# The last expert tiles are added to the output in two column halves instead of whole rows

## The chip, the core and the metric

The kernel runs on one core of a Trainium2 chip. The metric is the device time of one execution in microseconds (us). Engines are named as the profile names them: PE (TensorE matmul), PEld (its weight load), DVE (VectorE), ACT (ScalarE), POOL (GpSimd) and SP (SyncE); a `q` after a name (POOLq) is that engine's own instruction sequencer.

## What is computed

The reference is a two-layer graph network followed by a routed feed-forward layer, on x with 1250 rows of 1024 floats:

```python
x = x + gnn(layernorm(x), src, dst, ...)          # two SAGE layers over 40,000 edges
t = layernorm(x)
logits = silu(t @ rw1 + rb1) @ rw2 + rb2          # 8 experts
vals, idx = top_k(logits, 2)                      # 2 experts per row
w = softmax(logits, only the two chosen)
eh = silu(einsum('td,edh->teh', t, ew1) + eb1)    # hidden size 256
eo = einsum('teh,ehd->ted', eh, ew2) + eb2
out = x + t + sum over e of w[t,e] * eo[t,e]
```

So each of the 1250 rows gets two expert results added, 2500 (row, expert) pairs in all.

## The kernel before

The graph part runs first (functions `gnn_windows` and `after_layers`). When it is done, `after_layers` has written the normalised rows to a DRAM scratch `t_d` and the base value x + t to `out`. The rest is `moe`: it routes every row, packs the 2500 pairs into tiles of 128 slots that each belong to one expert, and works tile by tile. `NTILE` is 27, `always` is 20: tiles 0 to 19 are always worked, the rest under a runtime branch on `n_tiles`, the count of tiles that this input needs. `ends` is [23, 25, 27]: one branch for tiles 20 to 22, one nested in it for 23 and 24, one more for 25 and 26. In the profiled execution 23 tiles are worked (23 scatters, L1608), so the first branch is entered and the second is not.

For tile i the steps are:

- `gather(i)` (L1547, POOL): an indirect DMA reads 128 rows of `t_d`. It is issued three tiles ahead.
- `fetch(i)` (L1558, L1561): PE transposes the tile, ACT copies it out of PSUM.
- `first_layer(i)` (L1575, L1581): PE multiplies by the expert's first weights; DVE copies the hidden rows.
- `turn_hidden(i)` (L1588, L1590): PE transposes them, ACT applies bias and silu.
- `second_layer(i)` (L1597 to L1608): ACT scales the expert's bias row; for each of the two column halves (512 columns) PE runs its matmuls (L1602) and DVE writes `yo = ps * w + yb` for that half (L1607). Then POOL issues one indirect DMA (L1608) that adds the 128 rows of `yo` to rows of `out`, with `compute_op=ALU.add`; the row of each slot stands in `to[:, i]`. Slots that hold no pair have an index beyond `bounds_check` and move no row.

`yo` has two buffers, `yos[i % 2]`. Rows may be added to by two different tiles, so each scatter waits until the one before it has landed in `out`. The plan of tiles 4 and up is made once, in `plan_rest`: its call of `tokens_of` (L1405 to L1416) writes the columns 4 to 26 of `to` with one DVE instruction (L1416).

Program order decides the order on each engine: `section` (a loop over tiles) issues for tile i the gather of i + 3, the fetch of i + 1, the hidden transpose of i - 1, the first layer of i, then the second layer of i - 1. PE and ACT follow this order as written (`manual_schedule`); on POOL gathers and scatters form one queue, in order. A branch is taken by every engine by itself: L1654 is the line of the `If` on `n_tiles`, L1727 that of the `If` on `ok` after all tiles, which skips a second, general version of the whole kernel, and L1759 is the end of the kernel. A DMA of POOL signals its landing on one of eight semaphores, DMASW0 to DMASW7; POOL's DMAs from `gather(0)` on take them in turn, 0 to 7 and again from 0. Where a branch is not entered, the program has instructions on the other side that wait on semaphores the skipped side would have used, and raise them by as much as it would have (the record `INC_SWDGE_SEM`), so that both sides leave the same counts.

Of the kernel before, what the change touches and what calls it, by code (L numbers as in the profile page):

```python
# [14 lines left out]
I32 = mybir.dt.int32  # L15
AF = mybir.ActivationFunctionType
ALU = mybir.AluOpType
# [4 lines left out]
P = 128  # L22
# [7 lines left out]
def kernel(  # L30
# [21 lines left out]
    nc = tc.nc  # L52
    N, D = x.shape
# [12 lines left out]
    NTILE = (2 * N) // P + E  # L66
    assert R * 2 * EG == NE and R <= P and 2 * NB * WIN <= 512 and N > WIN
    rows = [min(P, N - b * P) for b in range(NB)]
# [70 lines left out]
    def tt(o, a, b_, op):  # L139
        nc.vector.tensor_tensor(o, a, b_, op)  # L140
# [912 lines left out]
    def moe():  # L1053
        st = ExitStack()
# [75 lines left out]
        sel_b = keep([P, NB_B + 1, E], F16)  # L1130
        beg_a, full_a = keep([P, E]), keep([P, E])
        ids, to, eid = (keep([P, NTILE], I32) for _ in range(3))
        w_slot = keep([P, NTILE])
        all_i = keep([P, 1], I32)

# [8 lines left out]
        group, ready = [], []  # L1144
# [63 lines left out]
        sums = SC[:, 2048:].rearrange("p (a n) -> p a n", a=4)  # L1208
# [186 lines left out]
        def by_slot(cols, nb, n):  # L1395

            ps = tpp.tile([P, 4, P], F32, name="tp").rearrange("p a b -> p (a b)")[:, :n]
            todo = [(c, b) for c in range(2) for b in range(nb)]
            for c, b in todo:
                r = at_row_a[:, c, b, :] if b < NA_B else at_row_b[:, c, b - NA_B, :]  # L1400
                nc.tensor.matmul(
                    ps, r, cols(c, b), start=((c, b) == todo[0]), stop=((c, b) == todo[-1])
                )
            return ps

        def tokens_of(at_tile, nb, i0, i1, take):

            n = i1 - i0
            tok = take([P, 2, nb, n], F16)
            tt(tok, at_tile, token[:, None, :nb, None].to_broadcast([P, 2, nb, n]), ALU.mult)  # L1410
            pi = by_slot(lambda c, b: tok[:, c, b, :], nb, n)
            nc.vector.tensor_scalar(ids[:, i0:i1], pi, -1.0, 0.0, op0=ALU.add, op1=ALU.max)
            to_f = take([P, n])
            nc.vector.tensor_scalar(to_f, pi, 0.0, float(4 * NP), op0=ALU.is_equal, op1=ALU.mult)
            tt(to_f, to_f, pi, ALU.add)
            nc.vector.tensor_scalar(to[:, i0:i1], to_f, -1.0, None, op0=ALU.add)  # L1416


        def weights(b0, nb, sel, take):
# [36 lines left out]
        def plan_first():  # L1456
            take = carver(scratch)
            choose(0, NA_B, sel_a, take)
            take = carver(scratch)
            rank = ranks(NA_B, sel_a, take)  # L1460
            hi_, lo_ = shifted(rank, take)
            nc.vector.tensor_copy(full_a, hi_[:, NA_B, :])
            nc.vector.tensor_copy(j[:, :NA_B], hi_[:, :NA_B, :])
            row = take([P, NA_B, E])
            nc.vector.tensor_copy(row, lo_[:, :NA_B, :])
            by_choice(row, 0, NA_B, rw[:, :, :NA_B], take)
            one_hot_rows(at_row_a, 0, NA_B)
            s = sums_before(full_a, take)
            nc.vector.tensor_copy(beg_a, s)

            til = take([P, NA_B, E])
            tt(til, j[:, :NA_B], full_a[:, None, :].to_broadcast([P, NA_B, E]), ALU.is_ge)
            stt(til, til, float(4 * NTILE), j[:, :NA_B], op0=ALU.mult, op1=ALU.add)
            tt(til, til, beg_a[:, None, :].to_broadcast([P, NA_B, E]), ALU.add)
            end = take([P, E])
            tt(end, beg_a, full_a, ALU.add)
            tw = take([P, 2, NA_B])
            by_choice(til, 0, NA_B, tw, take)
            at_tile = one_hot_tiles(tw, NA_B, 0, NT_A, take)
            tokens_of(at_tile, NA_B, 0, NT_A, take)  # L1480
            experts_of(0, NT_A, end, take)
            return at_tile, take

        def plan_rest():
# [40 lines left out]
            at_tile = one_hot_tiles(tw, NB, NT_A, NTILE, take)  # L1525
            yield
            tokens_of(at_tile, NB, NT_A, NTILE, take_l)
            experts_of(NT_A, NTILE, tot, take_l)
            yield at_tile
# [65 lines left out]
        def second_layer(i, e, hT):  # L1595
            yo, yb = yos[i % 2], ybs[i % 4]
            nc.scalar.activation(yb, yb, AF.Copy, scale=w_slot[:, i : i + 1])  # L1597
            for h in range(2):
                dc = slice(h * HALF, (h + 1) * HALF)
                ps = mm2.tile([P, 512], F32, name="ps2")  # L1600
                for q in range(KH):
                    nc.tensor.matmul(  # L1602
                        ps, hT[:, q, :],
                        w2_all[:, ds(e, 1), q * D + h * HALF : q * D + (h + 1) * HALF],
                        start=(q == 0), stop=(q == KH - 1),
                    )
                stt(yo[:, dc], ps, w_slot[:, i : i + 1], yb[:, dc], op0=ALU.mult, op1=ALU.add)  # L1607
            nc.gpsimd.indirect_dma_start(  # L1608
                out=out[:, :],
                out_offset=bass.IndirectOffsetOnAxis(ap=to[:, i : i + 1], axis=0),  # L1610
                in_=yo, in_offset=None, bounds_check=N - 1, oob_is_err=False,
                compute_op=ALU.add,
            )

# [2 lines left out]
        always = -(-2 * N // P)  # L1617
# [4 lines left out]
        def section(i0, i1, joined=True, until=None, middle=None):  # L1622

            for i in range(i0, i1):
                if i + 3 < NTILE and i > 1:
                    gather(i + 3)
                ahead = i + 1 < (until or i1)
                if ahead:
                    spread_bias(i + 1)
                    xTs[i + 1] = fetch(i + 1)  # L1630
                rest = None
                if i > i0 or joined:
                    turned = turn_hidden(i - 1, *held.pop(i - 1))
                    rest = lambda: second_layer(i - 1, *turned)

                early = rest if not ahead and until is None else None
                held[i] = first_layer(i, xTs.pop(i), middle or early)
                if rest is not None and early is None:
                    rest()

        def sections(i0, ends):
            last = held.pop(i0 - 1)

            def end_of_last():
                second_layer(i0 - 1, *turn_hidden(i0 - 1, *last))

            if not ends:
                end_of_last()
                return

            joined = i0 == always
            if not joined:
                end_of_last()
            with tc.If(n_tiles > i0) as more:  # L1654
                spread_bias(i0)
                xTs[i0] = fetch(i0)
                if joined:
                    held[i0 - 1] = last
                section(i0, ends[0], joined)
                sections(ends[0], ends[1:])  # L1660
            if joined:
                with more.Else():
                    end_of_last()
# [60 lines left out]

    gnn_windows()
    ok = moe()
    with tc.If(ok == 0):  # L1727
        gnn_any()
        moe()
# [34 lines left out]
```

## Time and profile before

| | us |
|---|---|
| median of 3 runs | 1120.42 |
| the 3 runs | 1119.36, 1120.42, 6438.05 |
| the profiled execution's own time | 1118.35 |
| its span, first to last instruction | 1116.6 |
| PE busy | 1089.5 (98%) |
| POOL busy | 313.6 (28%) |
| scatters (L1608): POOL busy, count | 36.5, 23 |
| last DVE result of the last tile, end | 1100.98 |
| last scatter, start on POOL | 1103.25 |

The two times at the bottom are counted from the span's start. The span covers the instructions of one execution; the execution's own time is 1.75 us more. A scatter's record on POOL (1586 ns in the mean) is the issue; its landing is found in the chain of waits and in the table of DMA issues.

### The profile page before, as it was taken

To read this page: it belongs to the slowest core of one execution; us is meant where nothing else is said; L and a number is where in the kernel's file an instruction comes from. 1 tells how busy PE (TensorE), PEld (TensorE's weight loads), DVE (VectorE), ACT (ScalarE), POOL (GpSimd) and SP (SyncE) were. 2 spreads that over 40 slices of the span, in tenths; PEclk is the share of its full clock that TensorE was granted. 3 is DMA by queue.
4 is the path that set the end of the run, shared out by engine and by line. 5 is a ranking of instruction groups with operands and counts; after the bars stand their busy time and mean duration, and the time that the engine had idled before them with its cause. 6 is when DMAs were issued, how large, how long until landed. Compare 5 with 4: busy or idle time off the path is not lost.

```text
span 1116.6 us, 13639 instructions
## 1 busy us (share of the span) xinstructions
PE 1089.5 (98%) x4881; PEld 809.9 (73%) x4881; DVE 472.9 (42%) x1172; ACT 218.3 (20%) x511; POOL 313.6 (28%) x407
## 2 busy tenths in 40 slices
PE   8999999999999999999999999999999999999993
PEld 7556556888888888888888888887544577676761
DVE  8767777763121245342234142455522263222221
ACT  4522222101111101110010000023111133333331
POOL 2999898500000000022002211254000013232321
PEclk9999999999999999999999999999999999999997
DMA  8011011010100020033004270343960456677762
GB/s 260 12 39 40 1 38 39 2 38 1 38 1 1 1 76 19 1 114 126 22 1 154 96 269 7 105 171 147 334 207 1 160 180 180 183 182 192 192 172 47
DMA packets 62320, 107.37 MB, mean 96 GB/s; under 512 B 8906, under 2 KB 35690, under 8 KB 62240
## 3 DMA queue, kind: packets, MB, share of 16 engines
q1 hardware_dynamic: 51392, 79.69, 20.9%
q0 software_dynamic: 7056, 23.88, 9.2%
q10 hardware_dynamic: 3792, 2.79, 0.8%
q8 instruction: 43, 0.70, 0.3%
q14 instruction: 37, 0.30, 0.1%
HBM read 80.74 MB, written 27.42 MB: 97 GB/s over the span
## 4 chain that ended last, share of the span: by engine, by line
PE 74%; DMA 16%; DVE 4%; issue 3%; ACT 1%; POOL 1%; SPq 0%; POOLq 0%; ACTq 0%; DVEq 0%
DMA out_dram<-L 13%; PE ps L532 12%; PE ps L460 11%; PE psb L664 11%; PE ps L760 8%; PE ps L664 8%; PE ps L568 8%; PE ps L1230 4%; PE ps L1244 3%; PE cnt L421 3%; PE ps L1183 2%; DMA b_p<-in_L_gnn_b_dram 1%; DMA more<-in_L_gnn_W_self_dram 1%; DVE xw L140 1%; PE ps L1575 1%
## 5 line engine op out<-in xcount | busy, mean ns | idle before, releaser
L413 POOL TENSOR_SCALAR ol<-lane,keys 125x128 f16<-125x128 f16 x280 | 171.0, 628 | 31.8 <-ACT keys L230 22.3
L460 PE MATMUL ps<-h0T,L 128*128 128x498 f32 (+2 forms) x384 | 146.0, 514 | 0.2 <-ACT h0T L309 0.2
L532 PE MATMUL ps<-L,h0T 128*128 128x256 f32 (+1 forms) x640 | 142.2, 379 | 0.8 <-DVE yl L387 0.8
L756 POOL TENSOR_TENSOR L<-L 128x512 f32<-128x512 f32 (+1 forms) x20 | 28.2, 1417 | 393.5 <-DMA L<-in_x_dram 393.4
L532 PEld LDWEIGHTS ps<-L,h0T 128*128 128x128 f32 (+1 forms) x640 | 118.3, 187 | 19.0 <-DVE yl L387 1.1
L460 PEld LDWEIGHTS ps<-h0T,L 128*128 128x128 f32 x384 | 67.2, 190 | 38.7 <-issue 34.7
L418 DVE TENSOR_SCALAR oh<-win,keys 125x240 f16<-125x240 f16 x320 | 81.1, 307 | 29.7 <-PE cnt L421 28.0
L1575 PE MATMUL ps<-xw,L 128*128 x368 | 84.1, 380 | 0.7 <-issue 0.7
L1602 PE MATMUL ps<-xw,L 128*128 x184 | 82.8, 593 | 0.5 <-ACT L L1590 0.5
L568 PE MATMUL ps<-C,yh 128*128 128x256 f32 (+2 forms) x240 | 81.7, 355 | 0.0
L568 PE MATMUL ps<-C,yl 128*128 128x256 f32 (+2 forms) x240 | 81.4, 353 | 0.0
L760 PE MATMUL ps<-zh,C 128*128 128x512 f32 (+1 forms) x200 | 79.5, 398 | 0.0
L760 PE MATMUL ps<-zl,C 128*128 128x512 f32 (+1 forms) x200 | 78.6, 393 | 0.0
L1575 PEld LDWEIGHTS ps<-xw,L 128*128 128x128 f32 x368 | 68.0, 190 | 9.5 <-issue 1.4
L440 DVE TENSOR_TENSOR C<-C,cnt 128x240 f32 x160 | 64.4, 402 | 12.9 <-DVE C L440 1.3
L1608 POOL DMA_INDIRECT out_dram<-L x23 | 36.5, 1586 | 118.2 <-DVE L L1607 62.0
L1547 POOL DMA_INDIRECT L<-t_d,L x26 | 25.5, 980 | 143.7 <-DVE L L140 122.9
L1602 PEld LDWEIGHTS ps<-xw,L 128*128 128x128 f32 x184 | 34.9, 190 | 34.9 <-issue 32.3
L1607 DVE SCALAR_TENSOR_TENSOR L<-ps,L 128x512 f32<-128x512 f32 x46 | 34.5, 751 | 53.1 <-PE ps L1602 53.1
L664 PE MATMUL ps<-L 128*128 128x256 f32 x240 | 56.2, 379 | 0.0
L387 DVE TENSOR_TENSOR yl<-ps,yh 128x256 fp32r<-128x256 f32 (+1 forms) x40 | 16.9, 423 | 92.3 <-ACT yh L386 92.3
L421 PEld LDWEIGHTS <-ol 125*128 125x128 f16 x320 | 31.0, 97 | 34.3 <-POOL ol L413 16.5
(237 smaller groups left out, 1558.1 us busy)
## 6 DMA issues: line engine op xcount, KB each, us to landing
xw<-in_L_ffn_ew_dram SPq DMA_DIRECT2D x16, 1024.0 KB, 11.2
L<-in_L_ffn_eb_dram SPq DMA_DIRECT2D x23, 512.0 KB, 4.7
L<-in_x_dram SPq DMA_DIRECT2D x20, 256.0 KB, 2.6
v_d<-L SPq DMA_DIRECT2D x18, 256.0 KB, 2.0
xa<-v_d SPq DMA_DIRECT2D x18, 256.0 KB, 7.2
t_d<-L SPq DMA_DIRECT2D x9, 512.0 KB, 3.8
out_dram<-xa SPq DMA_DIRECT2D x9, 512.0 KB, 4.0
L<-in_L_gnn_W_self_dram SPq DMA_DIRECT2D x4, 1024.0 KB, 5.3
```

What stands on the lines that cost most here:

```text
L413: nc.gpsimd.tensor_scalar(ol[:, c, :], lane[:GP], k, None, op0=ALU.is_equal)
L418: nc.vector.tensor_scalar(oh, win[:GP], keys[:, 0, i * GC + c, r : r + 1], None, op0=ALU.is_equal)
L421: nc.tensor.matmul(ps[:, i, :GW], ol[:, i * GC + c, :], oh, start=(c == 0), stop=(c == GC - 1),)
L440: nc.vector.tensor_tensor(to, to.bitcast(F32), ps[:, i, :GW].rearrange("p (k w) -> p k w", k=NB), ALU.add,)
L460: nc.tensor.matmul(ps[:, :n], w[:, k, (d % 2) * P : (d % 2 + 1) * P], h0T[:, k, c0 : c0 + n], start=(k == 0), stop=(k == KD - 1),)
L532: nc.tensor.matmul(ps[:m, :QW], hT[:, k, blk(b)], w[:, k, :], start=(k == 0), stop=(k == KD - 1))
L568: nc.tensor.matmul(ps[:, :n], part[: rows[k], k, (d % 2) * P : (d % 2 + 1) * P], C[: rows[k], k, c0 : c0 + n], start=(k == 0 and part is y ...
L664: nc.tensor.matmul(ps, rows_of(k), w[:, k, :], start=(first and k == 0), stop=(k == KB - 1), skip_group_check=not first,)
L760: nc.tensor.matmul(ps[:m], C[: rows[k], k, blk(b)], part[: rows[k], k, :], start=(k == 0 and part is yh), stop=(k == NB - 1 and part is yl),)
L1230: nc.tensor.matmul(ps, a_[:, k, :], b_[:, k, :], start=(start and k == 0), stop=(stop and k == KB - 1),)
L1575: nc.tensor.matmul(ps[:, :H], xT[:, k, :], w1_all[:, ds(e, 1), k * H : (k + 1) * H], start=(k == 0), stop=(k == KD - 1),)
L1602: nc.tensor.matmul(ps, hT[:, q, :], w2_all[:, ds(e, 1), q * D + h * HALF : q * D + (h + 1) * HALF], start=(q == 0), stop=(q == KH - 1),)
```

## The change

For the tiles 17 and up (`always - 3`) the one scatter of 1024 columns becomes two, of 512 columns each. `out` is viewed as 2500 rows of 512 columns, row 2r + h for half h of row r, and an index table `to_half` holds these row numbers. Each half is issued right after the DVE instruction that writes its half of `yo`. Two dependency groups, `sums0` and `sums1`, declare that scatters of different halves do not depend on each other, so each half waits only for the same half of the tile before. Tiles 0 to 16 scatter as before. Two more DVE instructions, once, fill `to_half` for tiles 4 to 26.

```diff
+        halves = st.enter_context(tc.tile_pool(name="halves", bufs=1))
+        to_half = halves.tile([P, 2, NTILE], I32, name="to_half")
...
             nc.vector.tensor_scalar(to[:, i0:i1], to_f, -1.0, None, op0=ALU.add)
+            if i1 > always - 3:
+                for h in range(2):
+                    nc.vector.tensor_scalar(
+                        to_half[:, h, i0:i1], to_f, 2.0, h - 2.0, op0=ALU.mult, op1=ALU.add
+                    )
...
                 stt(yo[:, dc], ps, w_slot[:, i : i + 1], yb[:, dc], op0=ALU.mult, op1=ALU.add)
-            nc.gpsimd.indirect_dma_start(
-                out=out[:, :],
-                out_offset=bass.IndirectOffsetOnAxis(ap=to[:, i : i + 1], axis=0),
-                in_=yo, in_offset=None, bounds_check=N - 1, oob_is_err=False,
+                if i >= always - 3:
+                    sent = scatter(to_half[:, h, i : i + 1], yo[:, dc], 2).ins
+
+                    tc.declare_no_dep(
+                        sent, group=f"sums{1 - h}", reason="other columns of the rows"
+                    )
+                    tc.add_to_no_dep_group(f"sums{h}", sent)
+            if i < always - 3:
+                scatter(to[:, i : i + 1], yo, 1)
+
+        def scatter(places, yo, parts):
+            return nc.gpsimd.indirect_dma_start(
+                out=out.rearrange("n (h c) -> (n h) c", h=parts),
+                out_offset=bass.IndirectOffsetOnAxis(ap=places, axis=0),
+                in_=yo, in_offset=None, bounds_check=N * parts - 1, oob_is_err=False,
                 compute_op=ALU.add,
             )
```

## The prediction

> **What bounds the kernel now.** First the page: PE is busy 98% of the span, so only work that lies after PE's last matmul, or that makes PE wait, can be moved by this change. I therefore read the end. The chain of waits for the last 60 us is made of scatters; its columns are start, duration and what ran (us); a `DMA out_dram<-L` row runs from a scatter's start on POOL to its landing:
>
> ```profile
> 1073.49 4.60 DMA out_dram<-L
> ...
> 1088.97 6.02 DMA out_dram<-L
> ...
> 1095.03 0.54 issue
> 1095.57 0.03 POOLq L1608
> 1095.60 0.19 issue
> 1095.79 6.70 DMA out_dram<-L
> ...
> 1102.54 0.49 issue
> 1103.03 0.05 POOLq L1654
> ...
> 1103.22 0.04 POOLq L1654
> 1103.27 1.53 POOL out_dram L1608
> ```
>
> Tile 20's scatter lands at 1094.99, tile 21's starts at 1095.79 (0.76 to 0.8 us after a landing) and lands at 1102.49, tile 22's starts at 1103.25. The timeline says what each was waiting for:
>
> ```profile
> 1098.57 0.75 DVE L1607 SCALAR_TENSOR_TENSOR L<-ps,L 128x512 f32<-128x512 f32 x1 [3.10 <-PE ps L1602]
> 1100.23 0.75 DVE L1607 SCALAR_TENSOR_TENSOR L<-ps,L 128x512 f32<-128x512 f32 x1 [0.91 <-PE ps L1602]
> 1103.25 1.55 POOL L1608 DMA_INDIRECT out_dram<-L  x1 [5.89 <-DMA out_dram<-L]
> ```
>
> The last sums are ready at 1100.98; where DVE is the releaser a scatter starts 0.28 us after it (tile 20: 1088.69 to 1088.97). So the last scatter stands 1103.25 - 1101.26 = 2.0 us late because of the scatter before it. These 2.0 us are what separate chains can win at the issue.
>
> The chain stops at the last scatter's issue, and the span goes on for 13.35 us. What happens there decides this case. The rows of the three lines that POOL's sequencer passes (count, durations in ns, first and last start) are:
>
> ```profile
> L1654 POOLq COMPARE_BRANCH  x2: 38/46/53, 1103.0 to 1104.6; - x2
> L1654 POOLq EVENT_SEMAPHORE  x2: 43/43/43, 1103.2 to 1103.3; - x2
> ...
> L1654 POOLq INC_SWDGE_SEM  x1: 1175/1175/1175, 1103.4 to 1103.4; - x1
> ...
> L1727 POOLq EVENT_SEMAPHORE  x6: 17/30/43, 1109.9 to 1110.4; - x6
> ...
> L1727 POOLq COMPARE_BRANCH  x1: 50/50/50, 1105.1 to 1105.1; - x1
> L1727 POOLq INC_SWDGE_SEM  x1: 1148/1148/1148, 1110.5 to 1110.5; - x1
> ...
> L1759 POOLq DRAIN  x3: 46/107/4077, 1111.6 to 1116.3; - x3
> ```
>
> Read in order of time: branch not entered at 1103.03, two waits and a semaphore raise while the scatter is still being issued, the branch on `ok` at 1105.13, then nothing for 4.8 us until 1109.93 (the far side of that branch; DVE shows 3.8 us on it, from 1101.7 to 1105.6), raises to 1111.6, a drain of 4.08 us, the end at 1116.6. The windows show this scatter's bytes moving from about 1105.0 to 1107.6. So **its landing lies under the 4.8 us after the branch**, with some 2 us to spare, and nothing waits for it. The span's end hangs on when POOL passes the branch, not on when the last sums land.
>
> **The change part by part.**
>
> *Index table.* Two more DVE instructions of 128x23, once, after the one at L1416 (0.18 us, 922.32). DVE stands idle for 1.13 us behind it, until PE's first layer ends. 2 x 0.18 = 0.36 us fits: 0; uncovered it would be 0.36 us.
>
> *Six more scatters.* Six tiles in halves: 12 issues in place of 6. Each has 128 rows as before, so I take the whole scatter's 1.59 us of POOL (half of it at the least, if the bytes counted). 6 x 1.59 = 9.5 us more on POOL, which sat idle for 5 to 6 us before each scatter. Behind them in POOL's queue stand the gathers of tiles 23 to 25, which this input does not work, so nobody waits for those. PE's order and waits and SP's queue are unchanged in the built program; a `yo` buffer is needed again two tiles (over 13 us) later. Cost: 0 on PE.
>
> *Half the bytes per row.* In the trace's packet records a row of 4,096 B takes 0.328 us in a scatter and 0.16 us in a gather, a scatter reading and writing `out`. Eight rows per DMA queue make 2.6 us; halves, by bytes, 1.3 us. So a half lands 6.0 - 1.3 = 4.7 us after its start. Tile 18 landed in 4.60 us: 95 of its 128 slots hold no pair and leave packets of 8 B. Tile 22 is like it, with 34 rows of 4,096 B. Five or six rows on the fullest queue save 5 x 0.16 = 0.8 us: 3.8 us. A rule speaks against that: the Trainium skill, "DMA: Bandwidth & Descriptors" (Anatomy of one DMA), puts a DMA of POOL at 2.0 us fixed, mostly the receipt of the last write, plus bytes / 436 GB/s. For the 34 rows it would save 0.16 us only, giving 4.4 us. No run here shows a half; I take 3.8, since the packet rows are this very operation. Lower end 2.9 (issue 1.55, one slow first packet 0.8, 0.5 to the semaphore), upper end 4.6 (no saving).
>
> *The two chains.* With 4.7 us (3.8 for tiles 18 and 22), 0.77 us from landing to start, 0.28 from DVE and 1.88 between two issues on POOL:
>
> | tile | half 0 | half 1 | set by |
> |---|---|---|---|
> | 17 | 1066.79 | 1068.67 | tile 16's landing, POOL |
> | 18 | 1072.25 | 1074.15 | landing, POOL |
> | 19 | 1079.33 | 1081.21 | DVE, POOL |
> | 20 | 1087.31 | 1089.19 | DVE, POOL |
> | 21 | 1092.77 | 1094.65 | landing, POOL |
> | 22 | 1099.60 | 1101.48 | DVE, POOL |
>
> The last issue moves from 1103.25 to 1101.48: **-1.8 us**, if it were all.
>
> *A wait that it adds.* The built program, POOL's instruction that raises the semaphores on the side not entered, before and after:
>
> ```
> L1654 ISA [waits DMASW4_49,DMASW3_49,DMASW5_49,DMASW2_49,DMASW1_49]
> L1672 ISA [waits DMASW4_49,DMASW5_49,DMASW3_49,DMASW6_49,DMASW2_49,DMASW7_49,DMASW1_49,DMASW0_49]
> ```
>
> The skipped tiles 23 to 26 used one gather and four scatters, five semaphores; now they use one gather and eight halves, all eight. POOL's DMAs take the eight in turn. Before, the last one (26 gathers and 23 scatters, the 49th) is on DMASW0, which is not in the list: no wait for it. Now 26 + 17 + 12 = 55 DMAs run and the last two are on DMASW5 and DMASW6, both in the list. POOL therefore **waits for the last half to land before it can reach the branch on `ok`**; queued behind that wait are the raise, the branch, the 4.8 us behind it and the drain, which all other engines await at L1759.
>
> Sum: half 1 of tile 22 lands at 1101.48 + 3.8 = 1105.28. From the second wait to the branch took 1105.13 - 1103.31 = 1.82 us before (raise 1.175 in it); with one more wait 1.9. The branch comes at 1107.2 instead of 1105.13: **+2.1 us**, and all behind it moves along: span 1116.6 + 2.1 = 1118.7. By the skill's rule (4.4) it would be +2.7. The ends of the landing give +1.1 (2.9) and +2.9 (4.6). The profiled execution's own time is 1118.35, 1.75 over its span; the median of the runs is 2.1 above that. I put the change on the median: 1120.42 + 2.1 = **1122.5 us**.
>
> **The rivals.**
>
> *Not slower: the landing stays covered.* If the waits on DMASW5 and 6 do not come on the path that runs, only the issue counts: -1.8, 1118.6 us. For it speaks the 2.0 us in the chain; against it the listing. Or the far side of the branch comes sooner, DVE's 3.8 us instead of POOL's 4.8, since no scatter moves beside it then: with a landing in 2.9 us that is +1.1 - 1.0, 1120.5 us. The point from which it decides: the landing would have to come by 1103.3, 1.8 us after the issue starts, for the wait to cost nothing; the issue alone takes 1.55.
>
> *Halves land no sooner than wholes* (6.0, 6.7 and 4.6 us for tiles 20, 21 and 22): half 1 of tile 20 lands at 1095.2, of tile 21 at 1095.97 + 6.7 = 1102.7, tile 22's starts at 1103.43, lands at 1108.0, branch at 1109.9: +4.8, 1125.2 us. The skill's fixed share speaks for it, the eight packets of 0.328 us against it.
>
> *Slower by over 2%*: 22 us. Five links from 1068.67 at (landing + 0.77) would have to push the last half to about 1123, a landing of over 10 us for each half. The longest of the whole scatters is 8.8 us. Only a collision of the two halves' rows could do it, and their columns are disjoint.
>
> **How the numbers follow.** Likeliest, the exposed landing: 0.55, own range 1120.5 to 1124.5. No saving in a half: 0.17, 1125.2. Landing covered or offset: 0.25, 1118.6 to 1120.5. The rest 0.03. The low end is the covered case with a little of the runs' own spread of 1 us, the high end the third case with as much: 1118.0 to 1126.5. Faster by over 2% is 22 us, more than the 15.6 us from DVE's last result to the end: 0.01. Slower by over 2%: 0.02. Within 2%, about what a measurement of this kernel can tell from no change: 0.97.
>
> **What would show it.** Chain: the last half starts near 1101.5, after POOL and not after a landing. Landings: halves of 3.5 to 4.8 us. L1672: POOL's waits start after the last landing, near 1105.3, not at 1103.2, and the branch after 1107. PE's last matmul unmoved, near 1100. If the branch on `ok` comes before 1105, the added wait is not there and the forecast is wrong; if the last half starts after 1103, the saving per half is.

## The result: 0.17% slower, and the profile after

| | before | changed |
|---|---|---|
| median of 21 runs each, us | 1119.1 | 1120.96 |
| ratio, 95% interval | | 1.0017, 1.001 to 1.0024 |
| profiled execution: own time, span, us | 1118.35, 1116.6 | 1120.84, 1119.1 |
| last DVE result to the end of the span, us | 15.58 | 17.19 |

One of the 21 runs of the kernel before took 6438 us; the median does not hang on it.

The loss is 1.9 us (1119.1 x 0.0017), by the interval 1.1 to 2.7. As far as the profiles tell, it lies in the end: PE's busy time is 1089.3 us against 1089.5, and from DVE's last result on, the changed kernel needs 1.6 us more. A second profile of each gave 15.77 and 17.09, a difference of 1.3. Before that point the profiled executions differ by 0.9 us, as executions of one kernel do (1100.98 and 1104.13 in the two of before), so the times below are counted from DVE's last result where it matters.

The last scatters in the timeline of the changed kernel (start, duration, engine, line, then in brackets the idle time before and what ended it):

```profile
1099.46 0.75 DVE L1614 SCALAR_TENSOR_TENSOR L<-ps,L 128x512 f32<-128x512 f32 x1 [3.09 <-PE ps L1609]
1100.48 1.55 POOL L1626 DMA_INDIRECT out_dram<-L,to_half  x1 [2.96 <-DVE L L1614]
1101.12 0.75 DVE L1614 SCALAR_TENSOR_TENSOR L<-ps,L 128x512 f32<-128x512 f32 x1 [0.91 <-PE ps L1609]
1102.34 1.55 POOL L1626 DMA_INDIRECT out_dram<-L,to_half  x1 [0.30 <-issue]
```

The first half starts when DVE has written it, the second as soon as POOL is free: 0.47 us after DVE's last result (1101.87), where the whole scatter stood 2.27 us after it. No landing holds them. So the two chains do what they were meant to. A half occupies POOL as long as a whole scatter, 1.55 us.

Then the three lines that POOL's sequencer passes (count, durations in ns, first and last start; L1672 was L1654, L1745 was L1727, L1777 was L1759):

```profile
L1672 POOLq EVENT_SEMAPHORE  x4: 17/42/43, 1102.1 to 1107.1; - x4
...
L1672 POOLq COMPARE_BRANCH  x2: 38/46/53, 1101.9 to 1108.5; - x2
...
L1672 POOLq INC_SWDGE_SEM  x1: 1280/1280/1280, 1107.2 to 1107.2; - x1
```

```profile
L1745 POOLq EVENT_SEMAPHORE  x6: 17/30/43, 1111.8 to 1112.3; - x6
...
L1745 POOLq COMPARE_BRANCH  x1: 50/50/50, 1109.0 to 1109.0; - x1
L1745 POOLq INC_SWDGE_SEM  x1: 1257/1257/1257, 1112.4 to 1112.4; - x1
```

```profile
L1777 POOLq DRAIN  x3: 46/107/4567, 1113.6 to 1118.8; - x3
```

Before, the waits at this place lay between 1103.2 and 1103.3. Now they reach from 1102.1 to 1107.1. Such a record starts when its wait is over: the first half lands at 1104.46 and the second record starts at 1104.49; the last half, started at 1102.34, lands at 1107.00 and the third record starts at 1107.03. Only then comes the raise. The branch on `ok` is passed at 1109.0, 7.2 us after DVE's last result (4.15 before). Behind it, it takes 2.8 us to the far side instead of 4.8; then come a raise of 1.26 us instead of 1.15, and a drain (`DRAIN`, POOL's longest record at the end of the kernel) of 4.567 us instead of 4.077.

### The profile page after: what moved, and what is told of

Read it like the earlier page. It is cut to its first block, busy times and chain, and to the rows that moved or that the text cites. A ratio compares the mean times of both kernels' runs of the same rounds, so it can differ in the third digit from the quotient of the medians.

```text
span 1119.1 us, 13658 instructions
## 1 busy us (share of the span) xinstructions
PE 1089.3 (97%) x4881; PEld 810.1 (72%) x4881; DVE 473.6 (42%) x1174; ACT 218.4 (20%) x511; POOL 323.2 (29%) x413
## 4 chain that ended last, share of the span: by engine, by line
PE 74%; DMA 14%; DVE 4%; issue 4%; POOL 2%; ACT 1%; POOLq 0%; SPq 0%; ACTq 0%; DVEq 0%
PE ps L532 12%; PE ps L460 11%; PE psb L664 11%; DMA out_dram<-L 10%; PE ps L760 8%; PE ps L664 8%; PE ps L568 8%; PE ps L1232 4%; PE ps L1246 3%; PE cnt L421 3%; PE ps L1185 2%; DMA more<-in_L_gnn_W_self_dram 1%; DMA out_dram<-L,to_half 1%; DMA b_p<-in_L_gnn_b_dram 1%; DVE xw L140 1%
## 5 line engine op out<-in xcount | busy, mean ns | idle before, releaser
L140 DVE TENSOR_TENSOR L<-L,ps 128x512 f32<-128x512 f32 (+1 forms) x30 | 18.0, 599 | 88.6 <-PE ps L1232 44.4
```

## The experiments

Each is a small edit of the changed kernel or of the one before. The condition under which a tile is halved stands in two places of `second_layer`; the diffs show the first.

### The wait alone, and the halves alone

**Halves where the tiles run, whole scatters where they are skipped:**

```diff
-                if i >= always - 3:
+                if always - 3 <= i < ends[0]:
```

> As the changed kernel (tiles 17 to 22 in halves), but the tiles 23 to 26, which this input skips, keep one whole scatter each. Their side then uses five semaphores again (DMASW7 and 0 to 3) and the last two halves (DMASW5 and 6) are not waited for. Theory (the changed kernel loses by the wait for the last half's landing): last half issued 0.5 us after DVE's last result as now, POOL's branch on ok 2.4 us after it (4.15 before, 7.2 in the changed kernel), the stretch after the branch back near 4.8 us because a scatter moves under it, end 1.8 us earlier than before: ratio near 0.9985. Rival (the loss comes from the six more DMAs: their issues, a longer drain of POOL): ratio stays at 1.001 to 1.002.

Measured: 1117.35 us, ratio 0.9983 (0.9968 to 0.9999); a second time 1117.34 us, 0.9983 (0.9971 to 0.9995).

```profile
1103.67 0.75 DVE L1614 SCALAR_TENSOR_TENSOR L<-ps,L 128x512 f32<-128x512 f32 x1 [0.91 <-PE ps L1609]
1104.89 1.55 POOL L1626 DMA_INDIRECT out_dram<-L,to_half  x1 [0.30 <-issue]
```

```profile
L1672 POOLq EVENT_SEMAPHORE  x2: 42/42/43, 1104.7 to 1104.8; - x2
L1672 POOLq INC_SWDGE_SEM  x1: 1293/1293/1293, 1104.8 to 1104.8; - x1
```

```profile
L1745 POOLq EVENT_SEMAPHORE  x6: 17/30/43, 1110.1 to 1110.6; - x6
...
L1745 POOLq COMPARE_BRANCH  x1: 50/50/50, 1106.7 to 1106.7; - x1
```

The scatters that run are the same as in the changed kernel. The waits are back at the last half's issue, 1104.7 to 1104.8, and the branch is at 1106.7, 2.3 us after DVE's last result (1104.42), 1.9 earlier than before. This gain of the chains now reaches the end. This kernel beats both: the code of tiles that never run decided the sign of the change. One number missed: the stretch behind the branch was 3.4 us (3.1 in the second profile), not 4.8. So in the two profiles the end after DVE's last result is 12.9 and 12.7 us long, 2.6 to 3.1 less than before: more than the chains alone give. The medians give 1.9 us (0.1 to 3.6).

**The reverse: whole scatters where the tiles run, halves in the skipped ones:**

```diff
-                if i >= always - 3:
+                if i >= ends[0]:
```

> The other half of the change alone: all tiles that run (0 to 22) scatter whole, and only the skipped tiles 23 to 26 are written in halves, so that all eight semaphores stand in the list that POOL waits for on the side not entered. No more DMAs run than before (49); the two DVE instructions of the index table run. Theory: POOL now waits for tile 22's whole scatter (4.6 us from its start), the branch on ok comes some 9 us after DVE's last result in place of 4.15, the stretch behind it shrinks to about 2.8 us as in the changed kernel, the end is 2.5 to 4.5 us later than before: ratio 1.002 to 1.004. Rival (a cost of the halves that run, not of the wait): ratio 1.000.

Measured: 1122.59 us, ratio 1.0031 (1.0018 to 1.0043).

```profile
1104.08 0.75 DVE L1614 SCALAR_TENSOR_TENSOR L<-ps,L 128x512 f32<-128x512 f32 x1 [0.91 <-PE ps L1609]
1107.25 1.55 POOL L1626 DMA_INDIRECT out_dram<-L  x1 [5.88 <-DMA out_dram<-L]
```

```profile
L1672 POOLq INC_SWDGE_SEM  x1: 1160/1160/1160, 1112.5 to 1112.5; - x1
```

```profile
L1745 POOLq EVENT_SEMAPHORE  x6: 17/30/43, 1117.0 to 1117.5; - x6
...
L1745 POOLq COMPARE_BRANCH  x1: 50/50/50, 1114.3 to 1114.3; - x1
```

As many DMAs run as before, in the same order; the only running work that is new is the two small DVE instructions of the index table. Yet POOL's raise waits for the whole scatter of 1107.25 to land (1112.5) and the branch comes 9.4 us after DVE's last result, with 2.8 us from it to the far side as in the changed kernel. The landing itself took 5.2 us, not the expected 4.6. The end after DVE's last result is 18.8 us long, 3.2 more than before. The two experiments together show the cause: by the medians the added wait costs about 3.5 us and the chains win about 2. The difference, 1.6, agrees with the 1.9 that the whole change costs, within the intervals.

### One chain of halves

The changed kernel without the two dependency groups:

```diff
-                    sent = scatter(to_half[:, h, i : i + 1], yo[:, dc], 2).ins
-
-                    tc.declare_no_dep(
-                        sent, group=f"sums{1 - h}", reason="other columns of the rows"
-                    )
-                    tc.add_to_no_dep_group(f"sums{h}", sent)
+                    scatter(to_half[:, h, i : i + 1], yo[:, dc], 2)
```

> The changed kernel without the two dependency groups: the halves are issued apart, but each waits for the half before it, so there is one chain of twelve links. Theory (the issue gains 1.8 us because two chains run side by side): links of 4.8 + 0.8 us from about 1066 put the last half near 1066 + 11 x 5.6 = 1127.6, 25 us later than in the changed kernel, PE waiting for free yo buffers: ratio about 1.02. Rival (PE sets the pace and the chains are hidden anyway): ratio within 0.002 of the changed kernel's 1.0017.

Measured: 1145.98 us, ratio 1.0229 (1.0203 to 1.0256). The timeline of its last scatters:

```profile
1113.59 1.55 POOL L1621 DMA_INDIRECT out_dram<-L,to_half  x1 [4.13 <-DMA out_dram<-L,to_half]
1119.30 1.55 POOL L1621 DMA_INDIRECT out_dram<-L,to_half  x1 [4.16 <-issue]
1124.83 1.55 POOL L1621 DMA_INDIRECT out_dram<-L,to_half  x1 [3.98 <-issue]
1129.46 1.55 POOL L1621 DMA_INDIRECT out_dram<-L,to_half  x1 [3.08 <-DMA out_dram<-L,to_half]
```

A link between full tiles is 5.5 to 5.7 us (4.8 to 5.0 to the landing, 0.8 to the next start), as expected, and a tile has two. The last link, of tile 22 with its 34 rows, is 4.6. Halves that wait for one another lose 26 us, so what gain there is comes from their independence.

The same with the skipped tiles whole, so without the wait at the end, run once:

> As the kernel with one chain of twelve halves, with the skipped tiles whole, so that the last half is not waited for. Its last scatter starts some 16 us after DVE's last result, when the other engines have long passed the branch on ok. It tells what stretches the time behind POOL's branch (4.8 us before, 2.5 to 2.7 where nothing else moved). If a scatter that moves under it does it: 3.5 to 4.8 us here. If the instruction reads of the other engines do it: 2.5 to 2.8 us here. By the wait's theory the time is 1 to 3 us under the one-chain kernel's 1146.

Measured: one run, 1145.89 us, so the time that it was to win was not seen. In the profile the end from the last scatter's start is 12.1 us instead of 15.9, but the last scatter itself stood 2.5 us later, which a single run does not explain. The stretch behind the branch was 2.8 us with a half moving under it:

```profile
L1740 POOLq EVENT_SEMAPHORE  x6: 17/30/43, 1136.9 to 1137.3; - x6
L1740 POOLq COMPARE_BRANCH  x1: 50/50/50, 1134.0 to 1134.0; - x1
```

So a half that moves does not lengthen it by itself, where the other engines passed the branch long before.

### Fewer and more halves

**Halves in tiles 20 to 22 alone:**

> Halves only in tiles 20 to 22, whole scatters in all others and in the skipped ones, so the last two halves (DMASW2 and 3) are not waited for. Theory: tile 19's whole scatter lands before tile 20's first sums are ready, so three tiles are enough: last half issued 0.5 us after DVE's last result, ratio near 0.9985 as with tiles 17 to 22. If POOL's drain at the end grows with the DMAs that ran (4.08 us at 49, 4.57 at 55), it is 4.3 us here at 52. Rival (the chains need a longer run-up): the last half waits for the one before it to land and comes 1 to 2 us after DVE's last result, ratio 1.000.

```diff
-                if i >= always - 3:
+                if always <= i < ends[0]:
```

Measured: 1116.92 us, ratio 0.998 (0.9965 to 0.9995). The time is the theory's, the start of the last half the rival's: 1.6 us after DVE's last result. Tile 20's first half waited for tile 19's whole scatter, its second half came behind that, and the chain of second halves (5.6 and 5.3 us to a landing, 0.75 to the next start) carried the delay to the last one:

```profile
1092.09 1.59 POOL L1626 DMA_INDIRECT out_dram<-L,to_half  x1 [4.51 <-DMA out_dram<-L]
1093.98 1.57 POOL L1626 DMA_INDIRECT out_dram<-L,to_half  x1 [0.30 <-issue]
...
1100.29 1.55 POOL L1626 DMA_INDIRECT out_dram<-L,to_half  x1 [0.96 <-DMA out_dram<-L,to_half]
...
1103.34 1.55 POOL L1626 DMA_INDIRECT out_dram<-L,to_half  x1 [1.50 <-DVE L L1614]
1106.31 1.55 POOL L1626 DMA_INDIRECT out_dram<-L,to_half  x1 [1.41 <-issue]
```

The run-up from tile 17 is worth about 1 us at the issue; three DMAs fewer give back part of it, since the drain is shorter:

```profile
L1777 POOLq DRAIN  x3: 46/107/4322, 1113.2 to 1118.1; - x3
```

Between the two no difference is measured.

**All running tiles in halves** (the condition `i < ends[0]`, and `to_half` filled for tiles 0 to 3 too):

> All tiles that run (0 to 22) in halves, the skipped ones whole; 72 DMAs of POOL run (55 with tiles 17 to 22). The last two halves are on DMASW6 and 7 and not waited for. Theory (POOL's drain at the end grows with the DMAs that ran, 4.077 us at 49, 4.322 at 52, 4.567 at 55, so 0.0817 each, and each of the two semaphore raises by 0.019 each): drain 4.077 + 23 x 0.0817 = 5.96 us, raises near 1.6 us, tail 2.0 us longer than with tiles 17 to 22 in halves: the gain is eaten, ratio 1.000. Rival (the drain does not follow the count): drain 4.6 us, ratio 0.998.

Measured: 1120.71 us, ratio 1.0006 (0.9994 to 1.0018).

```profile
L1672 POOLq INC_SWDGE_SEM  x1: 1630/1630/1630, 1102.5 to 1102.5; - x1
```

```profile
L1745 POOLq EVENT_SEMAPHORE  x6: 17/30/43, 1107.9 to 1110.5; - x6
...
L1745 POOLq INC_SWDGE_SEM  x1: 1608/1608/1608, 1110.5 to 1110.5; - x1
```

```profile
L1777 POOLq DRAIN  x3: 46/107/5955, 1112.2 to 1118.7; - x3
```

Drain and raises fall on the expected line, 5.955 us and 1.61 to 1.63 us. They account for 2.1 us over the kernel with 55 DMAs. There is a second loss that was not expected: the six waits on the far side take 2.6 us instead of 0.5, and in the trace a 16 KB read of instructions begins inside that gap. So in this profile the expected ratio came out for two reasons, not for the drain alone. How often the second one occurs is not shown: both together would make 4.2 us, and by the medians this kernel is 2.6 us slower than the one with 55 DMAs.

### What sets the stretch behind the branch

Here the stretch is counted from the end of the branch's record, 0.05 us after its start. Both kernels were profiled a second time:

> The kernel before once more, for a second profile of its end. If the 4.8 us behind POOL's branch on ok belong to this order of events, they come again within 0.5 us, and the raise of 1.15 and the drain of 4.08 us to the digit; if they are chance, they lie anywhere from 2.5 to 5 us.

> The changed kernel once more, for a second profile of its end. The last half lands 4 to 5 us after its start, POOL's branch on ok comes 7 us after DVE's last result, 2.5 to 2.8 us behind it, drain 4.57 us; a stretch of over 3.5 us would show that the short one of the first profile was chance.

Measured: 4.9 us in the second profile of before, 2.5 us in that of the changed kernel; raises and drains (1.148 and 4.077, 1.257 and 4.567 us) to the digit:

```profile
L1727 POOLq EVENT_SEMAPHORE  x6: 17/30/43, 1113.3 to 1113.7; - x6
L1727 POOLq COMPARE_BRANCH  x1: 50/50/50, 1108.3 to 1108.3; - x1
```

```profile
L1745 POOLq EVENT_SEMAPHORE  x6: 17/30/43, 1111.2 to 1111.7; - x6
L1745 POOLq COMPARE_BRANCH  x1: 50/50/50, 1108.6 to 1108.6; - x1
```

The difference came again, so it goes with the kernel. The kernel before with 64 unused POOL instructions in the part that is skipped:

```diff
     with tc.If(ok == 0):
+        for _ in range(64):
+            nc.gpsimd.memset(spare, 0.0)
         gnn_any()
```

> The kernel before with 64 more POOL instructions in the part that the branch on ok skips, so that nothing more runs but the far side of that branch lies 64 instructions further on, as far as in the changed kernel (65). If the place of the code among the instruction blocks makes the stretch behind the branch (4.8 and 4.9 us in two profiles of before, 2.7 and 2.5 in two of the changed kernel), it is 2.5 to 3 us here and the time 2 us lower: ratio 0.998. If it is the order of events (POOL branching just after the other engines, with no wait ahead), it stays at 4.5 to 5 us, ratio 1.000.

Measured: 1118.88 us, ratio 1.0004 (0.9992 to 1.0017), and a stretch of 4.6 us:

```profile
L1728 POOLq EVENT_SEMAPHORE  x6: 17/30/43, 1115.0 to 1115.4; - x6
...
L1728 POOLq COMPARE_BRANCH  x1: 50/50/50, 1110.3 to 1110.3; - x1
```

So the place of the far side's code, at least this shift of it, is not the reason. And the second measurement of the kernel with the skipped tiles whole, beside it:

> The kernel with tiles 17 to 22 in halves and the skipped tiles whole once more, beside the shifted one. Ratio 0.998 again, stretch behind the branch 3.4 us again if it belongs to this order of events, raise 1.27 to 1.29 us and drain 4.57 us to the digit.

Measured as told above, with a stretch of 3.1 us, raises of 1.29 and 1.26 us and a drain of 4.567 us. What is left, over all twelve profiles: 2.5 to 2.8 us where POOL branches 7 us or more after DVE's last result, long after the other engines (five profiles), 3.1 to 3.4 where it branches within 5 us of it, beside them, and over halves (four), 4.6 to 4.9 within 5 us and over a whole scatter (three). In both profiles of before, a 16 KB read of instructions begins about 2 us after POOL's branch; in both of the changed kernel it begins 1.1 us before it. Whether the other engines' reads, the rows of 4,096 B or both hold that read back stays open.

## Why the prediction was right

The forecast was +2.1 us; 1.9 were measured, from the mechanism that it named, and the two kernels that take the change apart moved in opposite ways as it demands. The forecast of the time itself, 1122.5 us, was 1.5 us too high, mostly because it stood on 1120.42, the median of 3 runs, where 21 gave 1119.1. The measurement was also finer than the forecast reckoned: it tells a change of 0.17% from none. From DVE's last result on, in the first profile of each kernel:

| step | forecast | before | changed | measured |
|---|---|---|---|---|
| to the last scatter's start | -1.77 | 2.27 | 0.47 | -1.8 |
| from there to the branch on `ok` | +3.82 | 1.88 | 6.70 | +4.8 |
| from the branch to its far side | 0 | 4.80 | 2.78 | -2.0 |
| from the far side to the end | 0 | 6.63 | 7.23 | +0.6 |
| sum | +2.05 | 15.58 | 17.19 | +1.6 |

*Index table, PE, POOL's room.* Right. The two DVE instructions lie before the next result of PE (1.0 us of idle time is left behind them), PE's busy time is unchanged, and a half does take a whole scatter's time on POOL.

*The two chains.* Right. With 0.9 us taken off, the starts of tiles 19, 20 and 22 are those of the table to 0.05 us. Tile 21's second half stood 0.4 us later. Tile 17 started 1.8 us earlier, since tile 16's scatter landed in 6.8 us instead of 8.2; it took 6.1 in the second profile of before, so this is spread and not the change.

*Half the bytes per row.* Right for full tiles: the eight halves of tiles 17, 19, 20 and 21 landed 4.7 to 5.2 us after their start (4.7 were forecast; whole, these tiles took 5.9 to 6.7), and a row of 2,048 B takes 0.178 us in the packet records against 0.328 for one of 4,096 B. So the rows decided: the median landing went from 6.0 to 4.8 us, 1.2 less. By the rule that the prediction cites, the Trainium skill, "DMA: Bandwidth & Descriptors" (Anatomy of one DMA), 2.0 us plus bytes / 436 GB/s, half the bytes would save 0.6 us by estimate; the trace does not agree.

Too small for the last tile, the term that counted: 3.8 us were forecast, 4.7 measured (4.0 for its first half). It was wrong in two ways. First, the 4.6 us from which it took its saving were tile 18's; tile 22's own whole scatter landed in 5.15 us before, and in 5.26 in the kernel with the wait alone. So halving saved 0.5 us, not 0.8. (The skill's rule, from the same 4.6, gave 4.4 and came nearer.) Second, it left out what else moves at that moment. The packet records show the last half's rows starting at 1104.46, but four of them only at 1105.83 to 1106.32, one behind the other, and a 16 KB read of instructions running from 1104.06 to 1105.84. The second profile shows the same (read until 1105.49, late rows from 1105.49), and so do both profiles of the kernel with the skipped tiles whole (1109.21 and 1109.20, 1106.15 and 1106.14). In the one chain of halves, where no such read runs and no other half moves, the same half landed in 4.1 us. That the read held those four rows up fits all five profiles; no experiment moved the read alone, so it is not shown.

*The added wait.* Right in place and order, as the lines of L1672 show. One reading beside it was too generous: before, the last scatter landed at 1108.40, so that 1.5 us were left to the far side of the branch, not some 2.

*The stretch behind the branch* was held at 4.8 us; it fell to 2.8, and why stays open. The rival of the covered landing had expected such a gain, 1.0 us, from a shorter stretch; the landing did not stay covered, but this part of it came true, twice as large.

*Drain and raise* were taken as fixed: they grew by 0.49 and 0.2 us (one raise of 0.11 lies before the branch, one behind it), since six more DMAs had run. This term was missing.

The three errors, +1.0, -2.0 and +0.6 us, mostly cancel. The sum is right by 0.4 us in this pair of profiles (0.7 in the second pair) and by 0.2 in the medians; its parts are not as good as that, and that the sum came so near is in part luck.

The other rivals: that halves land no sooner is refuted by the landings, and so is a loss of over 2%, which needed landings of over 10 us. Such a loss does come when the chains are joined (1.0229), a mechanism that the rival left out.

## What to carry to other kernels

At a kernel's end ask which engine passes the last instructions and what it waits for: a transfer that nobody waits for may be slow at no cost, and a change that makes it faster can also make somebody wait for it. Under runtime branches, code that is never entered can cost time, 3.5 us here: in this program the side taken waits for and raises the semaphores that the other side would have used, so count them before adding transfers there. Cut a serial chain only into parts that are declared independent, only in the last links that are exposed, and not in more transfers than that needs: by the estimate below each one lengthens the end by about 0.12 us here.

## What the runs showed of the hardware

- POOL's drain at the end grows with the DMAs that POOL issued in the run: 4.077 us at 49, 4.322 at 52, 4.567 at 55, 5.955 at 72, which is 0.082 us for each; the runs differ in the number of scatters alone. The raise (`INC_SWDGE_SEM`) at the end follows too: 1.148, 1.205, about 1.26, 1.608 us, 0.02 for each. By estimate from these figures, with two raises, an indirect DMA whose work is well hidden still costs about 0.12 us here.
- An indirect scatter-add of 128 rows takes POOL 1.55 to 1.61 us to issue, with rows of 4,096 or 2,048 B alike; a gather of 128 rows takes 0.97 to 1.01.
- A slot out of bounds leaves a packet of 8 B of about 0.01 us. Tiles with few rows land sooner, but not by much: before, tile 18 with 33 rows of 128 landed in 4.6 us and tile 22 with 34 in 5.15, full tiles near it in 5.9 to 6.7.
